# Inverse transforms by even and odd parts in a two-layer graph network

## The chip, the cores and the metric

The kernel runs on one core of a Trainium2 chip. The metric is the device time of one execution in microseconds (us); before the change three runs gave 1836.28, 1837.84 and 1840.70 us, median 1837.84. One execution more was recorded by the profiler, and every row of a trace shown here is from that one.

## What is computed

There are 128 graphs with 128 nodes and 256 channels, all in fp32. Layer 0 takes `h = relu(layernorm(x))` and builds, for each graph:

- a convolution branch over the node axis: a 1x1 convolution, batch norm and relu, then a convolution of 17 taps (padding 8) from 256 to 256 channels, batch norm, plus `h`, relu: `x_conv`;
- a message branch: three coordinates per node, `A = exp(-dist) * adj`, `x_nmp = A @ relu(h W_msg)`;
- a GRU cell on `[x_conv, x_nmp]` with state `h`, whose three gates give `(1 - z) * nn + z * h`, added to `x`.

Layer 1 is five small graph convolutions on the first 25 nodes.

```
h = _bn(_conv1d(h, conv2_w, 8), bn2_g, bn2_b, bn2_m, bn2_v)
x_conv = jnp.transpose(jax.nn.relu(h + xc), (0, 2, 1))
```

These two lines are what the change touches: the convolution of 17 taps, its norm, and the sum with `h`.

## The kernel before, in words

**The convolution as a product of spectra.** The 128 nodes with 8 of padding are 136 points, whose real transform has 136 numbers: 68 frequencies with two parts each (the second part of frequency 0 holds frequency 68). The head of the program (`weight_spectra`, `heads`) transforms weights and inputs. `spectral` then multiplies them, one frequency `p` at a time, for all 128 graphs: three products in place of four, with the difference of the weight spectra made by POOL (line 357) and the results put together by DVE (line 366) in a tile `ys`. Two frequencies are written at once, by ACT's queue (line 371), to DRAM: rows 0 to 127 of each graph to `yd`, the last 8 (four frequencies) to `yrd`. The spectra of the weights come from DRAM (`v`, line 338) through five buffers.

**The loop over blocks.** 32 blocks of four graphs follow. `gates(i)` issues the products of the GRU, unit by unit, seven products each by a Strassen-like scheme of quarters; after every product `between()` (here `step`) gives a turn to `beside_gates(i + 1)`, a generator that prepares the next block, and on other turns to the generators of layer 1. So the place of a `yield` in `beside_gates` decides between which products of the gates a piece of work stands. Every product takes one of eight PSUM banks from a ring (`bank`), so that a tile is given out again eight requests later, once its readers have ended. The order inside each engine follows the program closely; POOL's order in the spectral stage is written out by hand.

**The inverse transform of a block** stood in two functions of `beside_gates`:

- `short_rows(i)` takes four banks. The right half of each holds the distances of one graph (`pd`, line 565, five rows of `lt`). The left half, 256 columns, takes the product of the 8 residual rows of two graphs (`yr`, 16 rows at a row offset of 32 for each of four tiles) with a block-diagonal matrix `idr` (line 570), which opens the sum. ACT then takes the exponentials (line 574), DVE multiplies them by the adjacency (line 576).
- `conv_out(i, pss)` adds, for each half `o` of the channels and each pair `h` of graphs, two products of a graph's 128 rows by 128 channels (`ym`) with the 128x128 inverse matrix `idm` (line 588), lets DVE scale and add `ht` out of PSUM (line 591), and ACT take the relu (line 592). It yields after each half.

`load_y(i)` brings `ym` and four pieces of `yr` two blocks ahead on SP's queue. `ht` is the layer's `h`; nodes are stored in the order 0 to 63 and then 127 down to 64, so that a node of the first half and its mirror stand 64 apart.

The head of the program uses such mirrors already: `head_spectra` (line 279) transforms sums and differences of mirrored nodes, in products of 64 rows by 64 columns that lie on four quarters of the array.

Of the kernel before, what the change touches and what calls it, by code (L numbers as in the profile page):

```python
# [23 lines left out]
NR = LW - P  # L24
# [51 lines left out]
def gnn_kernel(ctx: ExitStack, tc: tile.TileContext, io, out0: bass.AP, out1: bass.AP):  # L76
# [35 lines left out]
    sc2, sh2 = bn[:, 1, 0, :], bn[:, 1, 1, :]  # L112
    bnr = hc.tile([P, 2, D], F32)
# [7 lines left out]
    def constants(pool):  # L121
# [28 lines left out]
        scales(1, V_BN2)  # L150
        nc.vector.tensor_add(brz, vec[:, V_IH:V_IH + 4], vec[:, V_HH:V_HH + 4])
# [8 lines left out]
    yd = dram.tile([B, P, D], F32, tag="yd", name="yd")  # L160
    yrd = dram.tile([B, NR, D], F32, tag="yrd", name="yrd")

# [167 lines left out]
    def spectral(bp, X, p_from, p_to, amid):  # L330

        x, base = X
        for p in range(p_from, p_to):
# [9 lines left out]
            y = ys[:, p % 2]  # L343
            ps = bank()
            if p == 0:
                for k, (u, w) in enumerate(((a, vr), (d, vi))):
                    for c in range(C):
                        nc.tensor.matmul(ps[:, k * D:(k + 1) * D], u[:, c], w[c], start=c == 0, stop=c == C - 1)
                nc.scalar.copy(y.rearrange("p k o -> p (k o)"), ps)
                continue  # L350
# [50 lines left out]
    with front as es:  # L401
# [70 lines left out]
        idm = gw.tile([P, N], F32)  # L472
# [53 lines left out]
    def load_y(i):  # L526
# [31 lines left out]
    def short_rows(i):  # L558

        yr, lt = loaded[i][1], lrs.pop(i)  # L560
        pss = [[bank() for _ in range(2)] for _ in range(C)]
        pd = [pss[b // 2][b % 2][:, H:H + N] for b in range(BB)]
# [3 lines left out]
        for o in range(C):  # L566
            for h, ps in enumerate(pss[o]):
                r0 = 32 * (2 * o + h)
                g = slice(r0, r0 + 2 * NR)
                nc.tensor.matmul(ps[:, :H], yr[g, :], idr[g, :], start=True, stop=False)  # L570
# [7 lines left out]
        return pss  # L578

    def conv_out(i, pss):  # L580

        ht = hts[i]
        ym = loaded.pop(i)[0]
        xc = wk.tile([P, C, T], F32, tag="xc", name="xc", bufs=2)
        for o in range(C):
            for h, ps in enumerate(pss[o]):
                for b in range(2):
                    nc.tensor.matmul(ps[:, b * N:(b + 1) * N], ym[:, 2 * h + b, o * P:(o + 1) * P], idm,  # L588
                                     start=False, stop=b == 1)
                v = slice(h * H, (h + 1) * H)  # L590
                nc.vector.scalar_tensor_tensor(xc[:, o, v], ps[:, :H], sc2[:, o:o + 1], ht[:, o, v], op0=ALU.mult, op1=ALU.add)  # L591
            nc.scalar.activation(xc[:, o, :], xc[:, o, :], AF.Relu, bias=sh2[:, o:o + 1])  # L592
            yield
# [583 lines left out]
def _spectral_constants():  # L1177
# [12 lines left out]
    inv = np.zeros((NP_, 2, P))  # L1190
# [10 lines left out]
    c, s = rows(_order() - (P - 1) / 2)  # L1201
    inv[0, 0], inv[0, 1] = c[0] / LW, s[NP_] / LW
    inv[1:, 0], inv[1:, 1] = 2 * c[f] / LW, -2 * s[f] / LW
    inv = inv.reshape(LW, P)
    idr = np.zeros((4, 32, 2, P))
    for b in range(2):
        idr[:, b * NR:(b + 1) * NR, b] = inv[P:]
# [96 lines left out]
```

## Time and profile before

| | |
|---|---|
| median of three runs | 1837.84 us (1836.28 to 1840.70) |
| profiled execution | 1838.96 us |
| its span, first to last instruction | 1837.1 us |
| granted TensorE clock, mean | 0.997 |
| head and forward transforms | about 0 to 253 us |
| products of the spectra (`spectral`) | about 254 to 431 us |
| loop over the blocks, rest of layer 1 | from 431 us to the end |
| products of line 588 | 512 instructions, 67.3 us busy |
| products of line 570 | 256 instructions, 19.8 us busy |
| products of line 565 | 256 instructions, 17.2 us busy |
| additions of line 591 | 128 instructions, 467 to 484 ns each |

The span lacks 1.9 us of the profiled execution's own time, which lie before the first and after the last instruction. PE is TensorE's matrix product and PEld its loading of weights, DVE VectorE, ACT ScalarE, POOL GpSimd, SP the engine that issues most of the transfers. A row of the trace names the line of the kernel, the tiles written and read (buffer numbers left out), shapes and a count; an fp32 product appears as two instructions. Lengths of matrix products overlap, so their pace is read from start to start.

### The profile page before, as it was taken

How to read it: one execution, taken by the hardware profiler on the slowest of the kernel's cores; microseconds unless marked ns; L12 is line 12 of the kernel's file. 1: busy time of each engine (PE TensorE's matmuls, PEld its weight loads, DVE VectorE, ACT ScalarE, POOL GpSimd, SP SyncE). 2: the span in 40 equal slices, each digit the busy share in tenths (PEclk: the TensorE clock that was granted, in tenths of full speed). 3: DMA queues.
4: the chain of work that ended last, by engine and by line, in shares of the span. 5: the costliest groups of instructions: out<-in, count | busy, mean ns of one | idle time of the engine just before them, and what ended most of it. 6: DMA issues, size and time to landing. Idle time of an engine off the chain costs nothing.

```text
span 1837.1 us, 34667 instructions
## 1 busy us (share of the span) xinstructions
PE 1810.6 (99%) x12552; PEld 1563.7 (85%) x12552; DVE 1357.2 (74%) x3328; ACT 734.4 (40%) x1624; POOL 790.5 (43%) x996
## 2 busy tenths in 40 slices
PE   8999999999999999999999999999999999999998
PEld 7777778887888888888788888888788888888786
DVE  7887857787878787877665787878656687877553
ACT  6666631112433434343434434333343434343343
POOL 5767775774344434443221344344312234443100
PEclk9999999999999999999999999999999999999999
DMA  8888889997533333343253433334334533342133
GB/s 302 330 326 326 330 292 309 350 309 228 146 83 74 85 84 78 86 108 91 63 114 102 121 85 85 74 82 115 79 82 97 140 71 90 79 101 50 42 94 119
DMA packets 279869, 267.46 MB, mean 146 GB/s; under 512 B 170870, under 2 KB 247371, under 8 KB 277651
## 3 DMA queue, kind: packets, MB, share of 16 engines
q1 hardware_dynamic: 274515, 247.32, 46.5%
q10 hardware_dynamic: 5184, 17.93, 2.4%
q8 instruction: 100, 1.64, 0.4%
q14 instruction: 70, 0.57, 0.1%
HBM read 168.84 MB, written 96.35 MB: 144 GB/s over the span
## 4 chain that ended last, share of the span: by engine, by line
PE 86%; DVE 4%; DMA 3%; issue 2%; ACT 2%; SPq 1%; POOL 1%; DVEq 0%; ACTq 0%
PE bank L708 44%; PE bank L365 6%; PE bank L1035 5%; PE bank L976 5%; PE bank L609 5%; PE bank L251 4%; PE bank L360 3%; PE bank L659 3%; PE bank L588 3%; PE bank L180 2%; PE bank L955 1%; DMA nt<-in_adjN_dram 1%; PE bank L885 1%; PE bank L279 1%; PE bank L237 1%
## 5 line engine op out<-in xcount | busy, mean ns | idle before, releaser
L721 POOL TENSOR_TENSOR u<-u,m 128x256 f32<-128x256 f32 x128 | 94.1, 735 | 461.7 <-ACT m L719 420.1
L708 PE MATMUL bank<-t,sw 128*128 128x256 f32 x1152 | 292.0, 380 | 0.7 <-DVE nn L723 0.4
L708 PEld LDWEIGHTS bank<-t,sw 128*128 128x128 f32 x1152 | 215.1, 191 | 33.5 <-issue 3.0
L708 PE MATMUL bank<-t,wih 128*128 128x256 f32 x768 | 200.3, 383 | 0.0
L708 PEld LDWEIGHTS bank<-t,wih 128*128 128x128 f32 x768 | 143.2, 190 | 29.3 <-DVE o L748 6.6
L251 PE MATMUL bank<-wc,ht 128*128 128x256 f32 x512 | 128.2, 394 | 4.8 <-ACT ht L238 4.8
L357 POOL TENSOR_TENSOR vs<-v 128x256 f32<-128x256 f32 x134 | 101.7, 783 | 52.7 <-DMA v<-vd 30.9
L708 PE MATMUL bank<-xc,wih 128*128 128x256 f32 x384 | 115.3, 382 | 1.6 <-ACT xc L592 1.6
L708 PE MATMUL bank<-xn,wih 128*128 128x256 f32 x384 | 114.9, 381 | 0.0
L1035 PE MATMUL bank<-w,hh 128*125 128x256 f32 (+9 forms) x480 | 114.6, 382 | 0.1
L708 PE MATMUL bank<-t,whh 128*128 128x256 f32 x384 | 114.6, 380 | 0.1
L251 PEld LDWEIGHTS bank<-wc,ht 128*128 128x128 f32 x512 | 90.8, 189 | 25.0 <-ACT ht L238 11.2
L708 PE MATMUL bank<-ht,whh 128*128 128x256 f32 x384 | 110.5, 381 | 0.7 <-DVE msg L628 0.4
L632 ACT ACTIVATE msg<-msg 128x512 f32<-128x512 f32 x64 | 36.8, 621 | 184.2 <-DVE msg L628 184.2
L592 ACT ACTIVATE xc<-xc,bn 128x512 f32<-128x512 f32 x64 | 46.2, 722 | 154.2 <-DVE xc L591 154.2
L1035 PEld LDWEIGHTS bank<-w,hh 128*125 128x125 f32 (+9 forms) x480 | 85.2, 179 | 18.5 <-DVE hh L981 1.2
L976 PE MATMUL bank<-ax,w 128*128 128x500 f32 (+9 forms) x352 | 94.5, 404 | 1.4 <-DVE xc L591 1.3
L726 DVE TENSOR_TENSOR u<-bank,u 128x256 f32<-128x256 f32 x128 | 53.3, 416 | 49.1 <-PE bank L708 48.6
L362 ACT COPY k<-bank 128x256 f32<-128x256 f32 x67 | 24.9, 372 | 145.8 <-PE bank L360 71.7
L708 PEld LDWEIGHTS bank<-xc,wih 128*128 128x128 f32 x384 | 72.3, 191 | 11.7 <-ACT xc L592 2.2
L189 ACT COPY sp<-bank 128x408 f32<-128x408 f32 (+1 forms) x160 | 66.9, 506 | 37.7 <-PE bank L180 37.5
L708 PEld LDWEIGHTS bank<-xn,wih 128*128 128x128 f32 x384 | 73.2, 191 | 10.1
(221 smaller groups left out, 4535.4 us busy)
## 6 DMA issues: line engine op xcount, KB each, us to landing
vd<-sp SPq DMA_DIRECT2D x16, 2176.0 KB
v<-vd SPq DMA_DIRECT2D x34, 1024.0 KB
w<-in_w_dram SPq DMA_DIRECT2D x40, 512.0 KB
ln<-in_x_dram SPq DMA_DIRECT2D x32, 512.0 KB
htd<-ht SPq DMA_DIRECT2D x32, 512.0 KB
yd<-ys ACTq DMA_DIRECT2D x32, 512.0 KB
ht<-htd SPq DMA_DIRECT2D x64, 256.0 KB
ym<-yd SPq DMA_DIRECT2D x32, 512.0 KB
```

The costliest lines, as they stand in the source:

```text
L189: nc.scalar.copy(dst, s)
L251: nc.tensor.matmul(pv[:, s, :], ht[:, c, (2 * h + s) * N:(2 * h + s + 1) * N], wc1[:, c, :], start=c == 0, stop=c == C - 1)
L357: nc.gpsimd.tensor_tensor(vs[:, c], vi[c], vr[c], op=ALU.subtract)
L360: nc.tensor.matmul(p1[:, :D], a[:, c], vs[:, c], start=c == 0, stop=c == C - 1)
L365: nc.tensor.matmul(ps[:, k * D:(k + 1) * D], u[:, c], w[c], start=c == 0, stop=c == C - 1)
L588: nc.tensor.matmul(ps[:, b * N:(b + 1) * N], ym[:, 2 * h + b, o * P:(o + 1) * P], idm, start=False, stop=b == 1)
L609: nc.tensor.matmul(ps[:, b, :], d[:, b * N:(b + 1) * N], w, start=True, stop=True)
L659: nc.tensor.matmul(ps[:, b * N:(b + 1) * N], msg[:, b, c * P:(c + 1) * P], e[:, b, :], start=True, stop=True)
L708: nc.tensor.matmul(ps, w, d, start=n == 0, stop=n == len(pairs) - 1)
L721: nc.gpsimd.tensor_tensor(got["u4"], got["u2"], got["m5"], op=ALU.add)
L976: nc.tensor.matmul(pv[:, q - q0, :], w1s[k5 + g][:, c, q * P:(q + 1) * P], xv[:, c], start=c == 0, stop=c == C - 1)
L1035: nc.tensor.matmul(ps[:n1, :D], hh[:, q, at:at + n1], w2s[k5 + g][:, q, :], start=q == 0, stop=q == HID // P - 1)
```

## The change

The even and the odd part of a real row of points can be transformed back apart. With mirrored nodes, the 64 cosine rows alone give the even part E and the 64 sine rows the odd part O, each for 64 node positions; a node of the first half is E - O, its mirror E + O. So the inverse matrix of 128x128 becomes two of 64x64.

- `yd` and `yrd` keep even and odd rows apart (`[B, 2, 64, D]` and `[B, 2, 4, D]`); `ys` is laid out to match, and a write takes, for each graph, two runs of 2 KB in place of one of 4 KB.
- `load_y` fills `ym` with 64 even rows above 64 odd rows; each piece of `yr` now holds the four residual rows of one part for four graphs.
- `edges` does the distances alone, with four banks of its own.
- `conv_out` takes four banks, one for each channel half and part, 256 columns for four graphs. The residual rows open the sums; then 32 products of 64 rows by 64 columns follow, whose operands and results lie in the four quarters in turn.
- Since E and O lie in different banks, DVE makes two additions for each: E with both halves of `ht`, then O with the negated and the plain scale (`nsc2`, a new constant), in place.
- `conv_out` no longer yields; `beside_gates` yields twice after it.

The line numbers of the changed program are six higher in this part. The diff, with the constants' building and declarations cut:

```diff
             if p % 2:
-                r = 2 * (p - 1)
-                to = yd[:, r:r + 4, :] if r < P else yrd[:, r - P:r - P + 4, :]
-                nc.scalar.dma_start(to.rearrange("g d o -> g (d o)"), ys.rearrange("p a k o -> p (a k o)"))
+                to = yd[:, :, p - 1:p + 1, :] if p < HN else yrd[:, :, p - 1 - HN:p + 1 - HN, :]
+                nc.scalar.dma_start(to.rearrange("g k a o -> g k (a o)"), ys.rearrange("p k a o -> p k (a o)"))
...
-        nc.sync.dma_start(ym, yd[g0:g0 + BB].rearrange("g r o -> r g o"))
+        nc.sync.dma_start(ym, yd[g0:g0 + BB].rearrange("g k r o -> (k r) g o"))
         for o in range(C):
-            for h in range(2):
-                r0, g1 = 32 * (2 * o + h), g0 + 2 * h
-                nc.sync.dma_start(yr[r0:r0 + 2 * NR, :],
-                                  yrd[g1:g1 + 2, :, o * P:(o + 1) * P].rearrange("g r o -> (g r) o"))
+            for e in range(2):
+                r0 = 32 * (2 * o + e)
+                nc.sync.dma_start(yr[r0:r0 + BB * NR, :], yrd[g0:g0 + BB, e, :, o * P:(o + 1) * P])
...
-    def short_rows(i):
+    def edges(i):
 
-        yr, lt = loaded[i][1], lrs.pop(i)
-        pss = [[bank() for _ in range(2)] for _ in range(C)]
-        pd = [pss[b // 2][b % 2][:, H:H + N] for b in range(BB)]
+        lt = lrs.pop(i)
+        pd = [bank()[:, :N] for _ in range(BB)]
         for b in range(BB):
             g = slice(32 * b, 32 * b + 5)
             nc.tensor.matmul(pd[b], lt[g, 0, :], lt[g, 1, :], start=True, stop=True)
-        for o in range(C):
-            for h, ps in enumerate(pss[o]):
-                r0 = 32 * (2 * o + h)
-                g = slice(r0, r0 + 2 * NR)
-                nc.tensor.matmul(ps[:, :H], yr[g, :], idr[g, :], start=True, stop=False)
...
-    def conv_out(i, pss):
+    def conv_out(i):
 
         ht = hts[i]
-        ym = loaded.pop(i)[0]
+        ym, yr = loaded.pop(i)
         xc = wk.tile([P, C, T], F32, tag="xc", name="xc", bufs=2)
+        pss = [[bank()[:, :H] for _ in range(2)] for _ in range(C)]
         for o in range(C):
-            for h, ps in enumerate(pss[o]):
-                for b in range(2):
-                    nc.tensor.matmul(ps[:, b * N:(b + 1) * N], ym[:, 2 * h + b, o * P:(o + 1) * P], idm,
-                                     start=False, stop=b == 1)
-                v = slice(h * H, (h + 1) * H)
-                nc.vector.scalar_tensor_tensor(xc[:, o, v], ps[:, :H], sc2[:, o:o + 1], ht[:, o, v], op0=ALU.mult, op1=ALU.add)
+            for e in range(2):
+                r0 = 32 * (2 * o + e)
+                g = slice(r0, r0 + BB * NR)
+                nc.tensor.matmul(pss[o][e], yr[g, :], idr[g, :], start=True, stop=False)
+        for o in range(C):
+            for b in range(BB):
+                for e in range(2):
+                    r = slice(HN * e, HN * e + HN)
+                    for q in range(2):
+                        v = slice(HN * q, HN * q + HN)
+                        nc.tensor.matmul(pss[o][e][v, b * HN:(b + 1) * HN], ym[r, b, o * P + HN * q:o * P + HN * q + HN],
+                                         idm[r, :], start=False, stop=b == BB - 1)
+            even, odd = (ps.rearrange("p (b j) -> p b j", j=HN) for ps in pss[o])
+            xv, hv = (t[:, o, :].rearrange("p (b s j) -> p b s j", s=2, j=HN) for t in (xc, ht))
+            for k in range(2):
+                nc.vector.scalar_tensor_tensor(xv[:, :, k], even, sc2[:, o:o + 1], hv[:, :, k], op0=ALU.mult, op1=ALU.add)
+            for k, sc in enumerate((nsc2, sc2)):
+                nc.vector.scalar_tensor_tensor(xv[:, :, k], odd, sc[:, o:o + 1], xv[:, :, k], op0=ALU.mult, op1=ALU.add)
             nc.scalar.activation(xc[:, o, :], xc[:, o, :], AF.Relu, bias=sh2[:, o:o + 1])
-            yield
         xcs[i] = xc
...
-            pss = short_rows(i)
-            yield
-            for _ in conv_out(i, pss):
-                yield
+            edges(i)
+            yield
+            conv_out(i)
+            yield
+            yield
             yield from x_nmp(i)
```

More of the change, by code (lines that the diff above doesn't have):

```diff
@@ L23 @@
 STEP = 3
-NR = LW - P
+NR = (LW - P) // 2
+HN = P // 2
 PARTS = [40, 40, 36, 12]
@@ L112, in gnn_kernel @@
     sc2, sh2 = bn[:, 1, 0, :], bn[:, 1, 1, :]
+    nsc2 = cst.tile([P, C], F32)
     bnr = hc.tile([P, 2, D], F32)
@@ L150, in constants @@
         scales(1, V_BN2)
+        nc.vector.tensor_scalar(nsc2, sc2, -1.0, None, op0=ALU.mult)
         nc.vector.tensor_add(brz, vec[:, V_IH:V_IH + 4], vec[:, V_HH:V_HH + 4])
@@ L159, in gnn_kernel @@
     vd = dram.tile([C, D // WCH, P, LW, WCH], F32, tag="vd", name="vd")
-    yd = dram.tile([B, P, D], F32, tag="yd", name="yd")
-    yrd = dram.tile([B, NR, D], F32, tag="yrd", name="yrd")
+    yd = dram.tile([B, 2, HN, D], F32, tag="yd", name="yd")
+    yrd = dram.tile([B, 2, NR, D], F32, tag="yrd", name="yrd")
     def taps_load(pool, c, q, queue, split=1, amid=None):
@@ L342, in spectral @@
             a, d = x[:, :, p - base, 0, :], x[:, :, p - base, 1, :]
-            y = ys[:, p % 2]
+            y = ys[:, :, p % 2]
             ps = bank()
@@ L348, in spectral @@
                         nc.tensor.matmul(ps[:, k * D:(k + 1) * D], u[:, c], w[c], start=c == 0, stop=c == C - 1)
-                nc.scalar.copy(y.rearrange("p k o -> p (k o)"), ps)
+                nc.scalar.copy(y, ps.rearrange("p (k o) -> p k o", k=2))
                 continue
@@ L471, in gnn_kernel @@
         gw = ctx.enter_context(tc.tile_pool(name="gw", bufs=1, side="right", reuse_waits="tile"))
-        idm = gw.tile([P, N], F32)
+        idm = gw.tile([P, HN], F32)
         wms = gw.tile([P, C, 2, MW], F32)
@@ L577, in short_rows @@
         A_s[i] = e
-        return pss
-    def conv_out(i, pss):
+    def conv_out(i):
         ht = hts[i]
-        ym = loaded.pop(i)[0]
+        ym, yr = loaded.pop(i)
         xc = wk.tile([P, C, T], F32, tag="xc", name="xc", bufs=2)
+        pss = [[bank()[:, :H] for _ in range(2)] for _ in range(C)]
         for o in range(C):
-            for h, ps in enumerate(pss[o]):
-                for b in range(2):
-                    nc.tensor.matmul(ps[:, b * N:(b + 1) * N], ym[:, 2 * h + b, o * P:(o + 1) * P], idm,
-                                     start=False, stop=b == 1)
-                v = slice(h * H, (h + 1) * H)
-                nc.vector.scalar_tensor_tensor(xc[:, o, v], ps[:, :H], sc2[:, o:o + 1], ht[:, o, v], op0=ALU.mult, op1=ALU.add)
+            for e in range(2):
[16 more added lines that the diff above has]
+                nc.vector.scalar_tensor_tensor(xv[:, :, k], odd, sc[:, o:o + 1], xv[:, :, k], op0=ALU.mult, op1=ALU.add)
             nc.scalar.activation(xc[:, o, :], xc[:, o, :], AF.Relu, bias=sh2[:, o:o + 1])
-            yield
         xcs[i] = xc
@@ L1189, in _spectral_constants @@
     fd = np.zeros((P, 2, NP_))
-    inv = np.zeros((NP_, 2, P))
     c, s = rows(np.arange(KW) - PAD)
@@ L1200, in _spectral_constants @@
         fd[k, 1, 0], fd[k, 1, 1:] = s[NP_], s[f].T
[L1201 to L1207, printed above, removed]
-    d = {"gt": gt.reshape(P, LW), "fd": fd.reshape(P, LW), "idm": inv[:P], "idr": idr.reshape(P, 2 * P)}
+    inv = np.zeros((2, NP_, HN))
+    inv[0, 0], inv[1, 0] = c[0] / LW, s[NP_] / LW
+    inv[0, 1:], inv[1, 1:] = 2 * c[f] / LW, -2 * s[f] / LW
+    idr = np.zeros((2, 2, 32, BB, HN))
+    for b in range(BB):
+        for e in range(2):
+            idr[:, e, b * NR:(b + 1) * NR, b] = inv[e, HN:]
+    d = {"gt": gt.reshape(P, LW), "fd": fd.reshape(P, LW), "idm": inv[:, :HN].reshape(P, HN), "idr": idr.reshape(P, 2 * P)}
     return {k: np.ascontiguousarray(v, dtype=np.float32) for k, v in d.items()}
```

## The prediction

> **What bounds the kernel now.** I read the head of the profile's page first, then the busy time by stage, then the instructions of the stages that the change touches in order of time. The head says which engine fills the span:
>
> ```profile
> span 1837.1 us, 34667 instructions
> PE 1810.6 (99%) x12552; PEld 1563.7 (85%) x12552; DVE 1357.2 (74%) x3328; ACT 734.4 (40%) x1624; POOL 790.5 (43%) x996
> ```
>
> TensorE (PE) is busy 99% of the span; VectorE (DVE) 74%. Since a busy PE need not be PE at its peak, I ask by stage. The windows list, for each stretch, its length and then the busy time of each engine, the granted clock, the DMA share and GB/s:
>
> ```profile
> 300.00:330.00 30.00, 30.00 (x140) 26.42 (x139) 20.64 (x36) 4.31 (x12) 17.01 (x24) 1.00 0.99 340
> 440.00:450.00 10.00, 8.71 (x69) 7.14 (x67) 7.29 (x17) 2.36 (x8) 2.71 (x4) 1.00 0.76 246
> 450.00:460.00 10.00, 8.63 (x45) 6.66 (x45) 8.79 (x26) 5.10 (x10) 4.01 (x5) 0.83 0.90 271
> 1000.00:1200.00 200.00, 200.00 (x1160) 178.60 (x1159) 155.92 (x374) 77.93 (x160) 80.76 (x99) 1.00 0.37 92
> ```
>
> In the block loop (1000 to 1200) PE never rests and DVE has 44 of 200 us left: whatever leaves PE's queue shortens the span one for one, and whatever is added to DVE is free while it delays no PSUM bank. Two places are tight: the products of the spectra (300 to 330), where the DMA engines are busy 99% while PE is full, and the first block (440 to 460), where PE idles and its clock drops to 0.83.
>
> The price of the edited code stands in the order of time on PE. The columns are start, length, engine, line, operation and count; one fp32 matmul of the program is two instructions.
>
> ```profile
> 1039.38 1.03 PE L708 MATMUL bank<-t,sw 128*128 128x256 f32 x4
> 1040.34 0.50 PE L565 MATMUL bank<-lt 5*128 5x128 f32 x8
> 1040.66 0.61 PE L570 MATMUL bank<-idr,yr 16*128 16x256 f32 x8
> 1041.21 1.13 PE L708 MATMUL bank<-t,wih 128*128 128x256 f32 x4
> 1042.17 0.59 PE L708 MATMUL bank<-xc,sw 128*128 128x256 f32 x2
> 1042.61 0.59 PE L708 MATMUL bank<-xn,sw 128*128 128x256 f32 x2
> 1043.04 1.05 PE L588 MATMUL bank<-idm,ym 128*128 128x128 f32 x8
> 1043.93 1.03 PE L708 MATMUL bank<-t,sw 128*128 128x256 f32 x4
> ```
>
> From start to start a full 128x256 instruction costs 0.216 us (0.43 for two), and the eight of L588 0.89: 0.111 each. They run twice per block. The same shape that the new code uses is already in the head of this kernel, the forward transform, 64 instructions of 64x64 weights on four tiles per call:
>
> ```profile
> 164.61 0.35 PE L279 MATMUL bank<-fd,ev 64*64 64x68 f32 x8
> 164.78 0.30 PE L279 MATMUL bank<-fd,h 64*64 64x68 f32 x8
> 164.90 0.30 PE L279 MATMUL bank<-fd,ev 64*64 64x68 f32 x8
> ...
> 165.49 0.30 PE L279 MATMUL bank<-fd,h 64*64 64x68 f32 x8
> 165.72 1.99 PE L251 MATMUL bank<-wc,ht 128*128 128x256 f32 x8
> ```
>
> Eight start in 0.12 us, 0.06 per round of four tiles; the call takes 1.11 us, of which 16 rounds are 0.96 and start and end 0.15. On DVE the adding out of PSUM comes in pairs, 0.87 us for two, so 0.40 from start to start:
>
> ```profile
> 1044.03 0.87 DVE L591 SCALAR_TENSOR_TENSOR xc<-bank,bn,ht 128x256 f32<-128x256 f32 x2
> ...
> 1047.12 0.86 DVE L591 SCALAR_TENSOR_TENSOR xc<-bank,bn,ht 128x256 f32<-128x256 f32 x2
> ```
>
> **What the Trainium skill says.** "TensorEngine Tiling (Array Packing)", Key Properties: changing the tiling mode drains TensorE. The trace agrees: L565 and L570 need 2 rounds of 0.111 and 2 of 0.216, together 0.65, but take 1.06 from the end of one stretch of full products (1040.24) to where the next would have had to start (1042.17 less four times 0.216, 1041.31). So entering, leaving and changing shape cost 0.41. The same page, PSUM Bottleneck: tiling speeds up TensorE and not the emptying of PSUM. That is this change's other side, and no line of before shows it under load. "DMA: Bandwidth & Descriptors", Why small descriptors are slow: some 3 cycles of overhead for each packet beside one per 32 bytes, so an estimate of 2% for a 2 KB piece against a 4 KB one; no run here shows it.
>
> **The change part by part, per block of four graphs (32 blocks).**
> *Main products.* Removed: 16 instructions of 0.111, 1.77 us. Added: 64 of 64x64 by 64 columns. In four tiles 16 rounds of 0.060 x 64/68 = 0.056, 0.90, and 0.15 for start and end as in the forward transform: 1.04 us. Half the arithmetic, but not half the time.
> *Edges on their own.* L565 no longer shares its change of mode with the residual rows. Alone: 0.10 in, its 0.32, 0.12 drain (the excess of L570's 0.55 over 0.43) and 0.10 on the next full product: 0.64.
> *Residual rows* still are four products of 16 rows by 256 columns, now ahead of the main products: 0.10 in, 0.55, then 1.04 of main products, 0.10 out: 1.79.
> *Sum.* Before 1.06 + 1.77 = 2.83, after 0.64 + 1.79 = 2.43: 0.40 saved, 12.8 us in 32 blocks. From both sides: with changes of mode at no cost beyond today's 0.41 it is 0.75 (24 us); with the extra 0.35 doubled, 0.05 (2 us). I take the middle, since every term is read off a row.
> *DVE.* Four additions become eight: 4 x 0.40 = 1.6 us per block, 51 us in all, taking the loop from 78% to about 82%. In the changed program's instruction order all eight stand together. Behind them queue the reads of gate product 7 and 4, then the rest of the nn unit. I cost this at nothing, with the cover named: eight PSUM banks. Counted from the start of the edges, PE ends the inverse products at 4.1, and takes four banks more (two products of 0.87, two of 1.3) until 8.4; only then does it ask again for the first of the four inverse banks. DVE gets there after the tanh of the first half and the subtraction that stand ahead in its order: product 3 at 2.3, its addition 2.9 to 3.3, the sum to 3.9, tanh to 4.7, subtraction to 5.4. The first bank is empty at 6.2, the last at 8.6, when PE needs it at 11.5. The cover is 2.2 us; beyond it PE pays each block.
> *Exponentials* wait for L565 alone, not for L570 (44 us of ACT idle, hidden): nothing. *Relu of xc* comes late by about 1.5 us in a block, but its first reader on PE is ten us off: nothing.
> *First block.* There the same eight additions are in the open: PE waits 1.57 us for xc. Four more additions of 0.47 stand ahead of the second half's relu, so that comes 1.9 us later, at a low clock: +2.
> *Results to DRAM.* The 34 writes of 512 KB go in pieces of 2 KB instead of 4 KB. Their queue takes 2.4% of the span's DMA time, 44 us, nearly all in this stage of some 175 us that is full; 2% of that is 1 us. But the loads come late: at 301.79 POOL gets its spectra and ends the first two subtractions at 303.2, 0.7 ahead of PE, which reads them at 303.91. Between 0 and +5; I take +0.5. The issues on ACT's queue stay 34. The loads of ym keep 1 KB pieces; yr stays four small loads per block, two blocks ahead, on SP's queue: nothing.
> *nsc2*, one tiny DVE operation in the head, hidden behind PE; idm of half the width: nothing.
> Total: -12.8 + 2 + 0.5 = -10.3. The profiled execution took 1838.96 us (span 1837.1), so 1828.7; the median of the three runs is 1.1 lower, so 1827.5.
>
> **The rivals.**
> Larger gain: the changes of mode overlap with the pulled-ahead weight loads and cost no more than now. For it: L279's first round loses only 0.05. Against: the 0.41 around L565. -24 + 2.5, 1816.
> Gain lost: each change of mode costs double, or the DMA of the spectra stalls PE by 5 us and the gain per block is 0.2: about 1838, no change.
> Slower, by PSUM: in the nn unit DVE reaches its eight additions 3 us later than I worked out (ACT's tanh behind two relus, or additions of the second layer in between), over the cover of 2.2 by 0.8. PE then waits 0.8 x 32 = 26 us: +15, 1853. It decides from the point where the delay exceeds the cover by 0.32 us in each block. For it: DVE is the second busiest engine and its order is fixed. Against: it still idles 3 to 4 us per block just after this place.
> The change doesn't do what it says: products that accumulate onto the residual rows run two at a time and not four. 32 rounds of 0.056 give 1.94 for 1.04, +0.9 x 32 = 29: 1856. Against: even and odd rows go to banks of their own, as in L279, which however never accumulates.
>
> **How the numbers follow.** Forecast as worked out 0.62, larger gain 0.13, gain lost 0.10, PSUM 0.10, tiles at half rate 0.05. 0.2% of this time, 3.7 us, is about what a measurement can tell from no change. The first two are faster, 0.75, the third the same, 0.10, the last two slower, 0.15. The low end, 1814, takes in the larger gain; the high end, 1842, takes in the lost gain and the mild part of the PSUM case, and leaves out its rest. The forecast's own range is 1820 to 1834.
>
> **What would show it.** On PE: the 64 instructions of a block starting within about 1.04 us, edges 0.64 and residual rows 0.65 with their entry. On DVE: eight additions of 0.4 in a row and a loop at 82%. In the waits: none of PE on the bank of an inverse product; one about 2 us longer on xc near 450 us. Wrong would be: PE's loop with idle time behind those eight additions, 64 instructions taking 2 us, or PE waiting for the spectra between 270 and 430 us.

## The result and the profile after

The changed kernel takes 1863.66 us (median of four runs, 1857.74 to 1867.26) against 1838.82 for the kernel before in the same session: a ratio of 1.013, 95% interval 1.0103 to 1.0156. It is 1.3% slower; 10 us faster was forecast. The profiled execution took 1857.74 us, the shortest of the four, with a span of 1856.0, so the two traces differ by 18.9 us and the medians by 24.8. The comparison below accounts for the 18.9; what the longer runs spend more was not recorded.

The head of the page of the changed kernel:

```profile
span 1856.0 us, 38119 instructions
PE 1819.9 (98%) x14088; PEld 1539.2 (83%) x14088; DVE 1419.5 (76%) x3457; ACT 737.1 (40%) x1624; POOL 798.5 (43%) x996
```

PE is still full, and by these shares alone nothing has happened. The chain that ended last, as shares of the span by engine, tells more. First the kernel before, then the changed one:

```profile
PE 86%; DVE 4%; DMA 3%; issue 2%; ACT 2%; SPq 1%; POOL 1%; DVEq 0%; ACTq 0%
```

```profile
PE 67%; DVE 18%; DMA 5%; issue 4%; ACT 2%; POOL 2%; SPq 1%; DVEq 0%; POOLq 0%; ACTq 0%
```

A fifth of the chain has gone from PE to DVE and DMA. By stage (length, then busy time of PE, PEld, DVE, ACT and POOL, clock, DMA share, GB/s), the changed kernel:

```profile
300.00:330.00 30.00, 30.00 (x141) 26.47 (x140) 21.15 (x36) 4.09 (x11) 16.89 (x24) 1.00 1.00 341
1000.00:1200.00 200.00, 199.55 (x1389) 172.50 (x1388) 163.62 (x389) 79.45 (x164) 79.42 (x95) 1.00 0.38 94
```

The spectra are as full of PE as before, so the smaller pieces of the writes cost nothing that shows. In the loop DVE is at 82% (163.62 of 200), as forecast, and PE rests for 0.45 of 200 us. The products themselves, in the order of time on PE in an ordinary block:

```profile
1124.97 0.50 PE L565 MATMUL bank<-lt 5*128 5x128 f32 x8
1125.40 1.13 PE L714 MATMUL bank<-t,wih 128*128 128x256 f32 x4
1126.48 0.70 PE L714 MATMUL bank<-xc,sw 128*128 128x256 f32 x2
1127.02 0.59 PE L714 MATMUL bank<-xn,sw 128*128 128x256 f32 x2
1127.54 0.71 PE L584 MATMUL bank<-idr,yr 16*128 16x256 f32 x8
1128.18 1.16 PE L591 MATMUL bank<-idm,ym 64*64 64x64 f32 x64
1129.28 1.13 PE L714 MATMUL bank<-t,sw 128*128 128x256 f32 x4
```

The 64 instructions take 1.10 us from their start to the next product, four at a time even onto sums that the residual rows have opened. But the full products near them are slow: four of `t,wih` take 1.08 where 0.97 is usual after a small one, two of `xc,sw` 0.54 where 0.43 is. These are waits too short to be listed as idle time of PE.

**Where the 18.9 us are.** The start of line 565 marks each block. I measure from one to the next; block n is the stretch that ends at the n-th start. Seventeen blocks are light, without work of layer 1: 3 to 9, 11, 17 to 21 and 27 to 30. In blocks 10, 12 and 22 layer 1 makes ready or begins a part.

| part of the span, us | before | after | difference |
|---|---|---|---|
| up to block 0 | 441.11 | 441.92 | +0.8 |
| blocks 1 and 2 | 59.49 | 59.79 | +0.3 |
| 17 light blocks | 614.03 | 623.28 | +9.3 |
| blocks 10, 12, 22 | 110.01 | 118.79 | +8.8 |
| blocks 13 to 16, 23 to 26 | 427.77 | 429.43 | +1.7 |
| block 31 and the end | 184.69 | 182.79 | -1.9 |

So two places need a cause: the light block, 36.12 us before and mostly 36.69 after, and the three blocks, 37.13, 36.46 and 36.42 before and 39.44, 39.33 and 40.02 after.

**The light block on DVE.** The kernel before, in order of time; in brackets the idle time before a row and who ended it:

```profile
1080.87 0.86 DVE L591 SCALAR_TENSOR_TENSOR xc<-bank,bn,ht 128x256 f32<-128x256 f32 x2
1081.66 0.68 DVE L753 TENSOR_TENSOR nn<-nn,o 128x512 f32<-128x512 f32 x1
1082.26 0.41 DVE L726 TENSOR_TENSOR u<-bank,u 128x256 f32<-128x256 f32 x1
1082.77 0.42 DVE L729 TENSOR_TENSOR nn<-u,bank 128x256 f32<-128x256 f32 x1
1083.13 0.89 DVE L759 TENSOR_TENSOR o<-ht,nn 128x512 f32<-128x512 f32 x1
1083.95 0.86 DVE L591 SCALAR_TENSOR_TENSOR xc<-bank,bn,ht 128x256 f32<-128x256 f32 x2
...
1097.94 0.68 DVE L762 TENSOR_TENSOR o<-o,z 128x512 f32<-128x512 f32 x1
...
1104.84 0.17 DVE L640 TENSOR_SCALAR lr<-lr 128x4 f32<-128x4 f32 x1
```

And the changed kernel:

```profile
1129.66 0.69 DVE L759 TENSOR_TENSOR nn<-nn,o 128x512 f32<-128x512 f32 x1
1131.15 0.69 DVE L765 TENSOR_TENSOR o<-ht,nn 128x512 f32<-128x512 f32 x1 [0.79 <-ACT nn L760]
1131.76 0.87 DVE L596 SCALAR_TENSOR_TENSOR xc<-bank,bn,ht 128x256 f32<-128x256 f32 x2
...
1134.89 0.41 DVE L732 TENSOR_TENSOR u<-bank,u 128x256 f32<-128x256 f32 x1
...
1146.79 1.21 DVE L768 TENSOR_TENSOR o<-o,z 128x512 f32<-128x512 f32 x1
...
1154.23 0.17 DVE L646 TENSOR_SCALAR lr<-lr 128x4 f32<-128x4 f32 x1
```

Before, two additions stood ahead of the sum `nn + o`, and two other operations out of PSUM (`u` and `nn`, lines 726 and 729) filled the time that ACT needs for the tanh between the sum and the subtraction. Now the first subtraction `o = ht - nn` stands in DVE's queue ahead of all eight additions and waits 0.79 us for the tanh. Behind them `u` of line 732 comes late, 9.92 us after the edges instead of 5.80. POOL's `nn` waits for it, the second sum on DVE for that, then its tanh on ACT, behind which ACT copies the `m` that POOL needs next; so POOL's run of eight operations for `t` begins 14.88 us after the edges instead of 13.85. POOL in the changed kernel:

```profile
1135.38 0.74 POOL L733 TENSOR_TENSOR nn<-u,m 128x256 f32<-128x256 f32 x1 [7.40 <-DVE u L732]
...
1139.85 0.73 POOL L688 TENSOR_TENSOR t<-ht 128x256 f32<-128x256 f32 x1
```

That run then lies beside more of DVE's operations: the second `o * z` takes 1.21 us instead of 0.68. At the end `lr`, which PE transposes for the next edges, is ready 29.43 us after the block's edges (1154.23 + 0.17 - 1124.97) instead of 28.55. PE took it up at 29.25 before, with 0.70 to spare; now that PE is quicker it is there earlier, and waits. The waits of the weight loads over the whole span (total, times, longest), before:

```profile
PEld bank L708 <- ACT m L711: 1.7, 4, 0.4
PEld bank L647 <- DVE lr L640: 1.4, 4, 0.7
```

and after:

```profile
PEld bank L653 <- DVE lr L646: 10.1, 20, 0.7
PEld bank L714 <- ACT m L717: 8.9, 23, 0.5
PEld bank L714 <- DVE ab L896: 8.2, 23, 0.5
```

About twenty blocks, each of the three. The first is for an operand. The other two are for a PSUM bank: `ab` and `m` are the readers of the bank that a product of line 714 is to write next, while that product's own operands, `xc` and the weights, had been used by earlier products already. In the light blocks none of the three is for a bank of the inverse products. (The list also has the weight load of the residual rows, `L584`, with 7.3 us in 22 waits. Two kernels below whose light blocks have no such loss have it too, with 7.6, so it isn't what costs.)

**Block 22.** SP's queue in the kernel before, then DVE:

```profile
1263.41 1.81 SPq L534 DMA_DIRECT2D yr<-yrd  x4
1265.26 0.70 SPq L906 DMA_DIRECT2D nt<-in_adjN_dram  x2
1266.84 0.39 SPq L530 DMA_DIRECT2D ym<-yd  x1
...
1268.55 0.72 DVE L913 TENSOR_TENSOR nt<-nt,ident 125x125 f32<-125x125 f32 x2 [1.91 <-DMA nt<-in_adjN_dram]
```

and in the changed one, with PE:

```profile
1279.59 2.68 SPq L536 DMA_DIRECT2D yr<-yrd  x4
1282.36 0.39 SPq L532 DMA_DIRECT2D ym<-yd  x1
1282.80 0.78 SPq L912 DMA_DIRECT2D nt<-in_adjN_dram  x2
...
1286.55 0.29 DVE L919 TENSOR_TENSOR nt<-nt,ident 125x125 f32<-125x125 f32 x1 [2.94 <-DMA nt<-in_adjN_dram]
...
1293.12 0.71 PE L615 MATMUL bank<-swm,t 128*128 128x130 f32 x4 [2.04 <-POOL t L689]
```

`nt` is a matrix of layer 1. Its load goes out 11.05 us after the block's edges (1271.75) instead of 8.20 (edges at 1257.06). Of the 2.85 us, 0.87 is that the four loads of `yr`, now in pieces of four rows from four graphs, take 2.68 us to issue instead of 1.81; 0.43 that `ym` now stands ahead; most of the rest came earlier, where SP took 1.79 instead of 0.61 us over the load of `dce` ahead of them; why it did is open. DVE waits in order, and in the end PE stands 2.04 us.

**Block 10** is another case. DVE of the kernel before, then DVE and PE of the changed one:

```profile
760.47 0.29 DVE L913 TENSOR_TENSOR nt<-nt,ident 125x125 f32<-125x125 f32 x1 [2.88 <-DMA nt<-in_adjN_dram]
```

```profile
765.46 0.29 DVE L919 TENSOR_TENSOR nt<-nt,ident 125x125 f32<-125x125 f32 x1 [1.97 <-DMA nt<-in_adjN_dram]
...
768.00 1.13 PE L665 MATMUL bank<-e,msg 128*128 128x128 f32 x8 [1.01 <-DVE xc L596]
```

Three loads of `nt` go out ahead of `yr` and `ym` here, 4.71 us after the edges instead of 4.39, and DVE waits less for one than before; yet the block is 2.3 us longer. The wait stands ahead of the additions in DVE's queue, and PE waits 1.01 us for a bank of the inverse products that the additions have not read yet. Such waits occur outside the light blocks only: 4.6 us in five places (the longest 1.90 and 1.35, in blocks 23 and 13), against 1.4 us in two places before.

### The profile page after: what moved, and what is told of

Its sections match the earlier page's. It is cut to its first block, busy times and chain, and to the rows that moved or that the text cites. A ratio compares the mean times of both kernels' runs of the same rounds, so it can differ in the third digit from the quotient of the medians.

```text
span 1856.0 us, 38119 instructions
## 1 busy us (share of the span) xinstructions
PE 1819.9 (98%) x14088; PEld 1539.2 (83%) x14088; DVE 1419.5 (76%) x3457; ACT 737.1 (40%) x1624; POOL 798.5 (43%) x996
## 4 chain that ended last, share of the span: by engine, by line
PE 67%; DVE 18%; DMA 5%; issue 4%; ACT 2%; POOL 2%; SPq 1%; DVEq 0%; POOLq 0%; ACTq 0%
PE bank L714 29%; PE bank L368 6%; PE bank L1041 5%; PE bank L982 5%; PE bank L254 4%; PE bank L363 3%; PE bank L665 2%; DVE xt L855 2%; DVE o L768 2%; PE bank L615 2%; PE bank L183 2%; DMA nt<-in_adjN_dram 2%; PE bank L961 1%; PE bank L282 1%; PE bank L591 1%
## 5 line engine op out<-in xcount | busy, mean ns | idle before, releaser
L733 POOL TENSOR_TENSOR nn<-u,m 128x256 f32<-128x256 f32 x32 | 24.9, 778 | 241.8 <-DVE u L732 241.8
L254 PEld LDWEIGHTS bank<-wc,ht 128*128 128x128 f32 x512 | 91.0, 190 | 24.8 <-ACT ht L241 11.3
L760 ACT ACTIVATE nn<-nn,vec 128x512 f32<-128x512 f32 x64 | 46.2, 722 | 128.3 <-DVE nn L759 128.3
```

Source lines behind the costliest of these rows:

```text
L254: nc.tensor.matmul(pv[:, s, :], ht[:, c, (2 * h + s) * N:(2 * h + s + 1) * N], wc1[:, c, :], start=c == 0, stop=c == C - 1)
L760: nc.scalar.activation(nn[:, q, :], nn[:, q, :], AF.Tanh, bias=vec[:, V_IH + 4 + q:V_IH + 5 + q])
```

## The experiments

Numbers of blocks are read as above; a light block's time is the commonest of its row.

The kernel before had medians of 1838.8 to 1839.9 us beside these runs; each ratio is to its own.

| kernel | median, us | ratio to before (95%) | light block | block 10 | block 12 | block 22 |
|---|---|---|---|---|---|---|
| before | 1838.82 | | 36.12 | 37.13 | 36.46 | 36.42 |
| changed | 1863.66 | 1.0130 (1.0103 to 1.0156) | 36.69 | 39.44 | 39.33 | 40.02 |
| before, 8 additions | 1838.45 | 1.0004 (0.9994 to 1.0014) | 36.12 | 38.93 | 36.14 | 36.13 |
| changed, 4 additions | 1839.15 | 1.0003 (0.9991 to 1.0016) | 35.83 | 38.68 | 39.46 | 39.16 |
| changed, two steps | 1858.77 | 1.0112 (1.0086 to 1.0138) | 36.67 | 39.42 | 36.68 | 37.37 |
| odd part by ACT and POOL | 1855.16 | 1.0098 (1.0070 to 1.0125) | 36.36 | 39.93 | 39.40 | 39.00 |
| tanh wait behind | 1850.89 | 1.0053 (1.0033 to 1.0073) | 35.83 | 40.18 | 40.37 | 41.01 |
| rows loaded later | 1862.07 | 1.0119 (1.0095 to 1.0143) | 36.68 | 36.66 | 37.23 | 38.65 |
| one visit | 1842.57 | 1.0015 (1.0004 to 1.0025) | 35.74 | 40.05 | 39.10 | 40.07 |
| before, edges apart, 8 additions | 1861.66 | 1.0117 (1.0101 to 1.0134) | 36.84 | 40.39 | 38.32 | 38.03 |
| changed, nt loads free | 1850.50 | 1.0064 (1.0048 to 1.0081) | 36.68 | 36.71 | 36.68 | 36.71 |
| one visit, nt loads free | 1825.37 | 0.9939 (0.9920 to 0.9957) | 35.74 | 35.75 | 35.93 | 35.74 |
| before, nt loads free | 1833.89 | 0.9972 (0.9964 to 0.9980) | 36.12 | 36.12 | 36.12 | 36.12 |
| changed, half of `t` | 1840.99 | 1.0009 (1.0000 to 1.0019) | 35.83 | 36.48 | 36.76 | 37.63 |

The first four of these experiments ask for DVE's work and its place alone. The load theory named in them is that the 1.6 us of four more additions cost what is seen; the place theory, that all eight standing in one step do. Totals outside every range that was named for them: the kernel with four additions lies between its two, the one with half of `t` 8 us below, the three with free `nt` loads 2 to 4 us below theirs, and two miss theirs by less than 1 us.

### Is it the work of the four more additions?

The kernel before with each addition made twice:

```diff
-                nc.vector.scalar_tensor_tensor(xc[:, o, v], ps[:, :H], sc2[:, o:o + 1], ht[:, o, v], op0=ALU.mult, op1=ALU.add)
+                for to in (wk.tile([P, H], F32, tag="spare", name="spare", bufs=2), xc[:, o, v]):
+                    nc.vector.scalar_tensor_tensor(to, ps[:, :H], sc2[:, o:o + 1], ht[:, o, v], op0=ALU.mult, op1=ALU.add)
```

> The kernel before, with each addition out of PSUM made twice (the first result goes to a spare tile): eight additions of 0.4 us per block for DVE as in the changed kernel, but in its four old places, and with the old products. Load theory (DVE's 1.6 us more per block is what costs): slower than before by 25 to 35 us, more than the changed kernel, since TensorE saves nothing here. Place theory (all eight in one step behind the wait for tanh is what costs): within 5 us of before.

Not one light block is longer (blocks 10 and 13 are, by 1.8 and 1.2 us, in the profiled execution, the slowest of twenty). DVE has the room for eight additions where no wait stands ahead of them, so the work alone is not the cause. The changed kernel without the additions of the odd part:

```diff
-            for k, sc in enumerate((nsc2, sc2)):
-                nc.vector.scalar_tensor_tensor(xv[:, :, k], odd, sc[:, o:o + 1], xv[:, :, k], op0=ALU.mult, op1=ALU.add)
```

> The changed kernel without its four additions of the odd part per block (the odd part is left out of the result). Load theory: the saving on TensorE shows, 8 to 12 us faster than before (about 1828). Place theory: the remaining four still stand in one place behind the wait for tanh, so only part of the loss goes: 1845 to 1855.

The light block falls to 35.83, which is what PE's new program takes when nothing is late: 0.29 less than before. The tanh wait still stands ahead of the four additions that are left:

```profile
1193.66 0.69 DVE L763 TENSOR_TENSOR o<-ht,nn 128x512 f32<-128x512 f32 x1 [0.79 <-ACT nn L758]
```

So the wait alone is not the cause either: the light block loses only where the wait and eight additions come together. The kernel as a whole gains nothing by it, because blocks 10, 12 and 22 stay long. That showed that there are two causes.

### Is it that all eight stand in one step?

```diff
             nc.scalar.activation(xc[:, o, :], xc[:, o, :], AF.Relu, bias=sh2[:, o:o + 1])
+            yield
...
-            conv_out(i)
-            yield
-            yield
+            for _ in conv_out(i):
+                yield
```

> The changed kernel with a yield after each half of the channels, as before the change: four additions in each of two steps. Load theory: as slow as the changed kernel, 1855 to 1868. Place theory: the gain appears, 1828 to 1840 (TensorE enters the tile mode once more per block, about 0.2 us).

Light blocks stay at 36.67. The subtraction that waits for the tanh is still first in DVE's order, now ahead of four additions, with the other four after the next sum. The step was not it. Blocks 12 and 22 are shorter, 36.68 and 37.37: here `nt` goes out behind the longer loads of `yr` but ahead of `ym`.

With the odd part taken off DVE:

```diff
-            for k, sc in enumerate((nsc2, sc2)):
-                nc.vector.scalar_tensor_tensor(xv[:, :, k], odd, sc[:, o:o + 1], xv[:, :, k], op0=ALU.mult, op1=ALU.add)
+            od = wk.tile([P, BB, HN], F32, tag="od", name="od", bufs=2)
+            nc.scalar.activation(od, odd, AF.Copy, scale=sc2[:, o:o + 1])
+            for k, op in enumerate((ALU.subtract, ALU.add)):
+                nc.gpsimd.tensor_tensor(xv[:, :, k], xv[:, :, k], od, op=op)
```

> The changed kernel with the odd part moved off DVE: ACT takes it out of PSUM with its scale, POOL adds and subtracts it. The result is complete. Load theory: 1826 to 1832, faster than both, as long as POOL's four operations of 0.7 to 0.9 us per block stay hidden. Place theory: 1845 to 1855.

36.36: better than 36.69 and not 35.83. POOL now has four operations more (2.79 us), which its `nn` stands behind, and its run for `t` begins 14.95 us after the edges, no earlier than in the changed kernel. This pointed from DVE's work to the time at which POOL's run begins.

### The tanh wait behind the additions

Only the place of the two subtractions is changed:

```diff
+        left = [2]
+
+        def differences():
+
+            left[0] -= 1
+            if left[0] == 0:
+                for q in range(C):
+                    tc.keep_in_program_order(nc.vector.tensor_sub(o[:, q, :], ht[:, q, :], nn[:, q, :]))
+            between()
+
-        unit(1, (2, 0, 1), z, (1, 6, 5, 7, 4, 2, 3), nxt)
-
-        for q in range(C):
-            nc.vector.tensor_sub(o[:, q, :], ht[:, q, :], nn[:, q, :])
+        unit(1, (2, 0, 1), z, (1, 6, 5, 7, 4, 2, 3), nxt, differences)
```

> The changed kernel with one thing moved: the two subtractions o = ht - nn, the first of which waits 0.79 us for ACT's tanh ahead of the eight additions, are kept behind the additions (after the second product of unit 1); all products, additions and transfers are those of the changed kernel. Queue theory (what costs is the tanh wait standing at the head of VectorE's queue, with eight additions behind it, so that POOL's nn and its t-operations start 1 us late): the light block falls from 36.69 to 35.9 us (35.83 was seen with four additions, 0.1 for what the other four add), 16 such blocks give 12.6 us, total 1846 us (1843 to 1850), the blocks where a part of layer 1 begins staying as long as they are. Rival, work theory (the eight additions in a run, or the new products on 64x64 tiles, cost this wherever the subtraction stands): 36.5 to 36.7 us a block, total 1855 to 1864.

DVE of this kernel, whose block begins at 1123.75:

```profile
1128.32 0.69 DVE L759 TENSOR_TENSOR nn<-nn,o 128x512 f32<-128x512 f32 x1
1128.93 0.87 DVE L596 SCALAR_TENSOR_TENSOR xc<-bank,bn,ht 128x256 f32<-128x256 f32 x2
...
1132.06 0.41 DVE L732 TENSOR_TENSOR u<-bank,u 128x256 f32<-128x256 f32 x1
...
1144.95 0.68 DVE L776 TENSOR_TENSOR o<-o,z 128x512 f32<-128x512 f32 x1
...
1151.85 0.17 DVE L646 TENSOR_SCALAR lr<-lr 128x4 f32<-128x4 f32 x1
```

The additions follow the sum at once, `u` comes 8.31 us after the edges instead of 9.92, POOL's run begins at 13.57, the second `o * z` takes 0.68, and `lr` is ready at 28.27. The light block is 35.83 with all eight additions and all the new products. For the light block the queue theory is shown: nothing but the place of the two subtractions, the first with its wait, is worth 0.86 us. On PE the 0.86 fall in four places: 0.21 in the products beside the edges (the bank that `ab` reads), 0.04 at the messages, 0.32 at `lr` and 0.28 ahead of the products with `ae` (the bank that `m` reads); all four vanish together. The total just missed its range (1843 to 1850) because other blocks got longer: 10, 12 and 22 by 2.8 us together, 1 and 2 by 3.6.

### Without a single 64x64 tile

The kernel before with its additions made twice, the edges in a visit of their own (a visit is a stretch of products that do not use the whole array) and the residual rows ahead of the inverse products, so that DVE's order becomes that of the changed kernel:

```diff
-        pss = [[bank() for _ in range(2)] for _ in range(C)]
-        pd = [pss[b // 2][b % 2][:, H:H + N] for b in range(BB)]
+        pd = [bank()[:, :N] for b in range(BB)]
...
+        pss = [[bank() for _ in range(2)] for _ in range(C)]
         for o in range(C):
             for h, ps in enumerate(pss[o]):
                 r0 = 32 * (2 * o + h)
                 g = slice(r0, r0 + 2 * NR)
                 nc.tensor.matmul(ps[:, :H], yr[g, :], idr[g, :], start=True, stop=False)
```

(the loop is moved from `short_rows` to `conv_out`, whose two yields now stand at its end; the doubled additions are those of the first experiment)

> The kernel before, its products of 128 rows by 128 columns and residual rows of two graphs unchanged, with every addition made twice (into a spare tile too) and two things of the change: the edges in a visit of their own, and the residual rows right ahead of the inverse products in one step. The scheduler then orders VectorE as in the changed kernel (nn + o, the subtraction that waits for the tanh, eight additions, u3), and SP as well (yr, ym, then nt). Queue theory: the light block rises from 36.12 to 36.9 to 37.2 us (0.87 of waits, up to 0.2 for the visit split), blocks 12 and 22 to about 39, total 1853 to 1862 us, without a single 64x64 tile. Rival (the 64x64 products and the even and odd parts are the cause): 36.1 to 36.4 us a block, total 1838 to 1845.

36.84, and a total as high as the changed kernel's. But its parts are not those expected. PE's products beside the edges:

```profile
1127.64 0.50 PE L564 MATMUL bank<-lt 5*128 5x128 f32 x8
1128.07 1.13 PE L710 MATMUL bank<-t,wih 128*128 128x256 f32 x4
...
1130.20 0.71 PE L584 MATMUL bank<-idr,yr 16*128 16x256 f32 x8
1130.85 2.05 PE L588 MATMUL bank<-idm,ym 128*128 128x128 f32 x16
```

Two blocks of this kernel without any wait (16 and 26) take 36.53: two visits cost 0.41 us more than one, where up to 0.2 was expected. Only 0.31 is waiting. `lr` is ready 29.57 us after the edges, a full microsecond later than in the kernel before, so the lateness on DVE is there without any new product; but PE, itself 0.62 later, asks for it at 29.87 and does not wait. The changed kernel, where PE is there at 29.22 (1153.33 + 4 x 0.216 - 1124.97), paid more for the same lateness because its products made PE earlier. Blocks 10, 12 and 22 are 3.6, 1.5 and 1.2 us longer than its light block, although the four loads of `yr` are those of the kernel before and take 1.81 us to issue; `ym` stands ahead of `nt` here too.

### One visit

In the changed kernel the residual rows are put back beside the edges:

```diff
-        lt = lrs.pop(i)
-        pd = [bank()[:, :N] for _ in range(BB)]
+        yr, lt = loaded[i][1], lrs.pop(i)
+        pss = [[bank() for _ in range(2)] for _ in range(C)]
+        pd = [pss[b // 2][b % 2][:, H:H + N] for b in range(BB)]
...
+        for o in range(C):
+            for e in range(2):
+                r0 = 32 * (2 * o + e)
+                g = slice(r0, r0 + BB * NR)
+                nc.tensor.matmul(pss[o][e][:, :H], yr[g, :], idr[g, :], start=True, stop=False)
```

(the same loop is taken out of `conv_out`)

> The changed kernel with the residual rows back beside the edges in one visit of TensorE (the edges in the right halves of the four banks of even and odd parts), the products on 64x64 tiles alone later. The scheduler then puts the eight additions ahead of the subtraction that waits for the tanh, and SP still issues ym ahead of the nt loads. Queue theory: the light block falls to 35.4 to 35.8 us (35.83 without operand waits, less up to 0.4 for a mode change saved), blocks 12 and 22 stay at 39 or more, total 1837 to 1845 us. Work theory (eight additions or 64x64 products cost in themselves): 36.3 to 36.6 us a block, total 1852 to 1860.

DVE takes all eight additions ahead of the subtraction here, which then no longer waits. The light block is 35.74, and in blocks 3, 16, 17, 26 and 27 it is 35.62 or 35.63. The second is 0.50 below the kernel before: 1.78 us of main products became 1.09, with 0.10 more on the product ahead of them and 0.10 on the one after. The queue theory fits again, with a total of 1842.57 inside its 1837 to 1845; blocks 10, 12 and 22 stay at 39 to 40.

### The late loads of layer 1

First the loads of `ym` and `yr` are issued after the gates of a block instead of ahead of them, so that SP reaches `nt` earlier:

```diff
             load_h(i + 2)
-            load_y(i + 2)
...
         gates(i, step, nxt, None if i else sums_ahead)
+        if i + 2 < NBLK:
+            load_y(i + 2)
```

> The changed kernel with the loads of ym and yr of block i + 2 issued after the gates of block i instead of before them; SP then issues the nt loads of layer 1 ahead of the four yr loads and ym, about 3.1 us earlier in the blocks where a part of layer 1 begins, and nothing moves on the other engines in the light blocks. Late-load theory (VectorE waits there 1.8 and 2.9 us in order for an nt load that SP issues late, and TensorE stands 2.3 to 3.6 us in the two blocks for POOL's and VectorE's operands): blocks 12 and 22 fall from 39.33 and 40.02 us to 36.7 to 37.5, the others stay (light block 36.7), total 1856 to 1860 us. Rival (the wait only moves to another load, or those blocks pay for the start of layer 1 itself): 39 to 40 us as now, total 1862 to 1866.

Block 12 fell as expected, block 22 by 1.4 of the 2.5 or more, and block 9 took over what block 10 had paid (40.16): loads of `nt` stand there too, and this time moved one block forward. In block 22 the loads of `nt` go out 8.04 us after the edges, as early as in the kernel before, and the block still pays 2.0 us over a light one; so the time of the load is not all of it. The total gained almost nothing and lies in the rival's range. The better test leaves out the one line that holds the `nt` loads in the program's order on SP, so that they go out whenever one of their eight buffers is free:

```diff
             ins = nc.sync.dma_start(nt[:n, :n], io["adjN"][j + 5, :n, :n])
-            tc.keep_in_program_order(ins)
```

> The changed kernel with one line left out, the one that keeps the nt loads of layer 1 in program order on SP: the first eight of them then go out around block 1 and the rest whenever one of the eight buffers comes free, so that none is left in blocks 9 to 12 and 22; the light blocks' order stays. Late-load theory (in those blocks VectorE waits in its queue for an nt load that SP issues late): blocks 10, 12 and 22 fall from 39.44, 39.33 and 40.02 us to that of a light block, 36.7, together 8.7 us, against 0 to 3 us more around block 1 or 2 for eight small additions there; total 1854 to 1858 us. Rival (those blocks pay for the start of layer 1 itself): 39 to 40 us as now, total 1862 to 1866.

Blocks 10, 12 and 22 become light blocks to 0.03 us. What they paid was the wait for that load with what it set off, and nothing that belongs to the start of layer 1. It is not free: blocks 1 and 2 take 66.25 us instead of 59.79, more than the 0 to 3 expected, since eight small additions and their loads now stand there; blocks 13 and 23 gave back 3.7.

### Both together, and the kernel before

> The kernel with one visit of TensorE for edges and residual rows, and the nt loads free as well. Both causes (the queue of VectorE in the light blocks, the late loads in blocks 10, 12 and 22) are then gone: light block 35.6 to 35.8 us, blocks 10, 12 and 22 as well instead of 40.05, 39.10 and 40.07, 12 us off 1842.6, 0 to 3 back around block 1: total 1829 to 1834 us, ratio 0.994 to 0.997. If blocks 10, 12 and 22 pay for something else, 1838 to 1845.

```profile
span 1822.5 us, 38084 instructions
PE 1796.0 (99%) x14088; PEld 1535.0 (84%) x14088; DVE 1408.6 (77%) x3457; ACT 738.8 (41%) x1624; POOL 808.3 (44%) x996
```

1825.37 us, ratio 0.9939 (0.9920 to 0.9957): faster than both kernels, with every one of the new products and additions in it.

> The kernel before with the nt loads free. It loses 1.0, 0.3 and 0.3 us in blocks 10, 12 and 22 against a light block: late-load theory, those 1.6 us go and 0 to 3 come around block 1, total 1836 to 1840 us, light block 36.12; so that what the kernel of the run before gains on this one comes from the products.

The kernel before gains 5 us by the same line (1833.89). Its light block stays at 36.12. So the products on 64x64 tiles are worth 1833.89 - 1825.37 = 8.5 us where nothing takes them back.

### Half of POOL's run

```diff
-                gate_inputs(i + 2, (2,))
+                ts[i + 2] = {2: ts[1][2]}
```

> The changed kernel, tanh wait and all eight additions where they are, with half of GpSimd's work beside VectorE left out: the four differences of the hidden state ht are not computed for blocks 2 on (the gates take those of block 1), so GpSimd's run of eight operations in a light block, 14.9 to 22.5 us after the edges, becomes four. Theory of the shared slowing (the 0.79 us of the tanh wait reaches TensorE only because GpSimd's run starts 1 us later and then lies beside VectorE's o * z, 1.21 us instead of 0.68, and xn differences, 0.94 instead of 0.53): lr is ready 0.9 us earlier, before TensorE asks for it, the light block falls from 36.69 to 35.8 to 36.0 us, total 1849 to 1853 us (16 to 19 blocks by 0.7 to 0.85). Theory of the plain delay (the 0.79 us in VectorE's queue alone is what TensorE sees): the light block stays at 36.4 to 36.7, total 1858 to 1864.

The tanh wait is still 0.79 us, and yet the light block is 35.83. The second `o * z`, whose block begins at 1151.72:

```profile
1172.02 0.68 DVE L768 TENSOR_TENSOR o<-o,z 128x512 f32<-128x512 f32 x1
```

With half of POOL's run gone the wait does not reach PE. That is weaker than it looks: DVE is ahead from the start of the block (the wait ends 5.33 us after the edges instead of 6.18), and `lr` is ready 27.0 to 27.4 us after them, earlier than in any other kernel here. So it shows that a shorter run frees DVE enough, not that the loss takes its way through the run, nor how it divides between the wait and the sharing. Blocks 10, 12 and 22 fell as well, to 36.5 to 37.6, with the order and the length of SP's loads as in the changed kernel; so what a late load costs there depends on DVE's room as well. The total went below what was expected.

## Why the prediction was wrong

**The step that failed first: "I cost this at nothing, with the cover named: eight PSUM banks."** Behind it stands the opening rule that "whatever is added to DVE is free while it delays no PSUM bank". The place was right. The text has the tanh and the subtraction ahead of the eight additions and works out when the banks come free; the trace has the last bank free 10.0 us after the edges (1134.50 + 0.47 - 1124.97) instead of 8.6, still ahead of the 11.5 given there for PE, and in a light block PE never waits on a bank of the inverse products. But the cover was worked out for these four banks alone. What stands behind the additions in DVE's queue is `u`, then POOL's `nn`, POOL's run for `t`, and at the end `lr`; `lr` had 0.70 us to spare, became 0.88 later, and PE's own gain made the demand earlier. Of the 0.86 us, 0.32 are at `lr` and 0.49 at the banks of `ab` and `m`, which DVE's lateness frees late. The text named "the reads of gate product 7 and 4, then the rest of the nn unit" as queued behind and did not ask who waits for those. Cost: 0.86 us in a light block, 14.2 in the seventeen (623.28 less 17 x 35.83).

**The second: "yr stays four small loads per block, two blocks ahead, on SP's queue: nothing."** Two blocks ahead they are early for PE; but in blocks 12 and 22 they are in front of `nt`. Their issue grew from 1.81 to 2.68 us, `ym` moved ahead of `nt`, and these two blocks paid 6.5 of the 8.8 us. With the `nt` loads free all three blocks pay nothing. How the 6.5 divide is open. Over their light blocks they pay 2.6 and 3.3 us in the changed kernel; with the short loads of `yr` and `ym` ahead of `nt` they pay 1.5 and 1.2, with the long ones and `nt` ahead of `ym` 0.0 and 0.7, with `nt` back at its old time 2.0 in block 22, and with more room on DVE 0.9 and 1.8. In block 10, with 2.3 of the 8.8, this step is not the cause, since the loads of `nt` go out ahead of `yr` there; the wait for `nt` was in the kernel before already, and with the additions behind it reaches a bank of the inverse products.

**The sum on PE: right in kind, its size 0.29 for 0.40.** Edges alone were put at 0.64. Measured in the kernel with the tanh wait behind: 0.43, with 0.10 on the product after and 0.10 on the one ahead, 0.63. The conv part was put at 1.79: the residual rows take 0.64 instead of 0.55, probably since the change from their tiles to the 64x64 ones costs as well, and the main products 1.10 instead of 1.04; with 0.10 in and 0.10 out that makes 1.94. The saving is then 2.83 - 2.57 = 0.26 by these rows, 0.29 by the blocks. The 0.41 us that a second visit cost agree with what the Trainium skill, "TensorEngine Tiling (Array Packing)", Key Properties, says of a drain at each change of mode. Seventeen light blocks would have saved 4.9 us; with the waits they lost 9.3.

**First block, +2:** the 1.57 us that PE waited there for `xc` is no longer in the list of waits; the span up to block 2 grew by 1.1. **Results to DRAM, +0.5:** PE waits for spectra once, 1.03 us at 257.59, ahead of the first write at 262.08. The products of the spectra begin 1.42 us later than before (254.97 and 253.55) and block 0 only 0.81, so the writes cost nothing that shows.

**The rivals.** "Tiles at half rate" lay nearest in number, 1856, by chance: it is refuted by the 1.10 us for 64 instructions. "Slower, by PSUM", at 1853, had DVE late behind the tanh, and DVE was 1.4 us later than worked out; but PE waits on the inverse banks in five places only, 3.2 us more than before, and not in each block. The "gain lost" did not name either cause.

## What to carry to other kernels

When work is added to an engine in front of others, follow everything queued behind it to its last reader, across engines, and write down the slack of each; the banks that the added work itself reads are only one of the things that can be late. A faster engine eats such slack from the other side, so a lateness that was harmless becomes a wait. A load that is early for its own reader still stands ahead of others in its queue, and an engine that takes its queue in order turns one late transfer into a stop for everything behind.

## What the runs showed of the hardware

DVE and POOL slow each other. An operation of DVE with two operands of 128x512 takes 0.68 us alone and up to 1.21 beside POOL's run, one of 128x256 0.41 and up to 0.95; POOL's own take 0.73, 0.91 or 1.18. The Trainium skill, "SBUF — State Buffer", section "SBUF: two separate sides", says that a DVE operation with two SBUF inputs and a POOL operation that reads SBUF take an exclusive lock on a shared pair of ports, and that the other one waits for the whole instruction. The trace agrees as far as both become longer, and with half of POOL's run left out DVE's were 0.68 again. The longest of both lengths grow by about the same 0.53 us, which fits a wait for the ports better than a shared rate; it is less than a whole operation of POOL's (0.73 or more), as it would be where part of that had passed, but no run here shows when a port was held.

In the kernel before, a second visit to small tiles cost 0.41 us although its products were the same. Products on four 64x64 tiles ran four at a time while adding to sums opened by products of another tile shape: 16 rounds in 1.10 us with that change.
